# One core, a depthwise convolution and an attention-and-FFN layer: the main stage's order by a place per task, the last product with 128 weight columns, and the first pixels loaded ahead of the build

## The chip, the core and the metric

One core of a Trainium2 chip runs the whole kernel. A core has a tensor engine for matrix products (PE in the profile; its weight loads are listed apart, as PEld), a vector engine (DVE), a scalar engine (ACT), a general engine (POOL) and an engine that only issues transfers (SP). ACT and POOL issue transfers too. Each engine has its own instruction list and works through it in order; the engines meet through semaphores. Sixteen DMA engines move data between DRAM and the on-chip memory (SBUF). The tensor engine writes into eight PSUM banks, which DVE and ACT read.

The metric is device time in microseconds for one execution, the median of three runs.

## What is computed

The input is `x`, 64 images of 55 x 55 pixels with 96 channels. Cut to what matters:

```python
# layer 0: a depthwise 25 x 25 convolution of which 9 x 9 taps less the centre are kept (every third row and column)
lat = conv_general_dilated(x, kernel * mask, strides (1, 1), 'SAME', feature_group_count=96)
x = lat * x + bias + x

# layer 1: tokens t = x as (64, 3025, 96)
n = layernorm(t)
h = relu(bn1(n @ w1.T))                    # 96 -> 192
X = fft(h over the 3025 tokens, ortho)
xr = relu(X.real * rd - X.imag * id + rb)  # rd, id: diagonals, per channel
xi = relu(X.imag * rd + X.real * id + ib)
y = ifft(xr + 1j * xi, ortho).real
t = t + bn2(y @ w2.T)                      # 192 -> 96
# FFN with quantised values: products of fp8 (5, 2), sums rounded to fp16
n = layernorm(t)
h = relu(q16(q16(q8(n) @ q8(W1).T) + q8(b1)))        # 96 -> 384
t = t + q16(q16(q8(h) @ q8(W2).T) + q8(b2))          # 384 -> 96
```

## The kernel before

It has two stages that follow one another.

**The convolution stage** begins with a build. `taps` and a table of selections `sel` are loaded, and 56 groups of small products (L205) make banded weight matrices out of them: one set for the first 48 channels, in `toep` (copied by ACT, L214), one for the other 48, in `later` (copied by DVE, L215). `later` is written to a DRAM scratch `tb` (L217) and comes back into `toep` half-way. Only then, on SP's queue behind the six `tb` transfers, are the first pixels loaded (`load`, L229 to L235, called at L304). Then twelve groups follow, listed at L223 to L225: a half of the channels, a row offset `r` (tiles: 4, 3 and 3) and a half of the images `bh`. Each group goes through its 48 channels in six steps of eight; `compute` multiplies (L253), DVE forms `(lat + 1) * x` (L261), POOL adds the bias (L271). There are six output buffers `buf`. `stores` gives the DMA issues that write a finished buffer to the DRAM scratch `t1`: large ones from ACT's queue (in the last group from SP's too) and small ones from POOL's. Stores are issued a few per step (L326), or at once where the next group needs the buffers (L315).

**The main stage** handles the 64 images one by one as `sequence(b)`, several of them in flight. One sequence is 289 tasks, of which 73 are the tensor engine's:

- load `t` (L549), statistics (L560), layernorm (`layernorm_tasks`), scale (L574), transpose (`pa`, L587, 7 tasks), first product (`ph`, L609, 13 tasks), relu, first transform over 121 tokens (`pf`, L624, 13 tasks), copy, then to DRAM `gd` and back as `gt`;
- the transform's second factor (`dft_r`, `px`, L692, 6 tasks of 32 products with 50 x 64 weights), ACT's three passes (L709), DVE's four (L718) and POOL's two (L725); `project` (`pd`, L767 and L777, 4 tasks of 32 products), `inverse_k1` (`pe`, L797, 4 tasks of 16 products), copies, through DRAM `ed` and back as `e2`;
- the inverse's last factor (`py`, L859, 5 tasks), residual and statistics, layernorm, quantise, transpose in fp8 (`pq`, L913, 7 tasks), up (`pu`, L936, 9 tasks), cast, bias and relu on DVE (L945, L948), quantised to fp8 `hq` by ACT (L960), down (`pw`, L981, 5 tasks of 15 products whose weights are 121 columns of `hq`), cast on ACT (L990), bias on DVE (L995), residual on POOL (L1001) and store.

`px`, `pd` and `pe` are products on a part of the array (64 x 64, or 128 x 64); all others use it whole. An fp32 product is two instruction pairs in the profile, a weight load and a matmul each.

The order of the tasks is set before the program is built. Each `task` has an engine, a cost in us and a place: a formula of the sequence number and of what it is (`at`, `bo`, `co`, `fo`). `ordered` plays the tasks through in time: a task is ready when its predecessors have ended and its buffers are free (`bufs` has their number: 5 of `t`, 4 banks in `psn`, 2 double banks in `psw`), and of the tasks that can start on an engine at nearly the same time the one with the lower place is taken, unless one with a place over `NEAR` higher is ready sooner. For the tensor engine a change of the array's form costs `SWITCH`. What comes out is the order of instructions of each engine, SP included; at run time only the semaphores decide when each one runs.

Of the kernel before, what the change touches and what calls it, by code (L numbers as in the profile page):

```python
# [11 lines left out]
F32 = mybir.dt.float32  # L12
# [9 lines left out]
NTOK = R * R  # L22
# [19 lines left out]
NOB = 6  # L42
SU = 21
# [8 lines left out]

@with_exitstack
def conv_attn_hybrid(ctx, tc, a, out, t1, tb, gds, eds):
# [21 lines left out]
    with ExitStack() as cx:  # L76
# [9 lines left out]
        later = lp.tile([128, CHH, NE * TQ], F32, tag="later", name="later")  # L86
# [47 lines left out]
        for of in (toep, later):  # L134
            nc.gpsimd.memset(of[:, :, : 2 * TQ], 0.0)
            nc.gpsimd.memset(of[:, :, 16 * TQ :], 0.0)
# [61 lines left out]
        for j0 in range(0, TQ, 5):  # L198
            nj = min(5, TQ - j0)
            for e in range(2, 16):  # L200
# [14 lines left out]
                nc.vector.tensor_copy(later[:, :, cols], src[:, CHH:])  # L215
        for c0 in range(0, CHH, CC):
            nc.sync.dma_start(tb[:, c0 : c0 + CC], later[:, c0 : c0 + CC])  # L217
        first.close()

        ob = cx.enter_context(tc.tile_pool(name="c_ob", bufs=NOB))
        groups = [(0, r, bh) for r, bh in ((0, 0), (1, 0), (0, 1), (1, 1), (2, 0), (2, 1))]  # L223
        halfway = groups[-1]
        groups += [(1, r, bh) for bh in range(BH) for r in range(NR)]  # L225
        steps = [(n, c0) for n in range(len(groups)) for c0 in range(0, CHH, CC)]
        xts, bufs_ = {}, {}

        def load(n, c0):  # L229
            half, r, bh = groups[n]  # L230
            c1 = half * CHH + c0
            for m in range(NTS[r]):
                x = xp.tile([128, CC, NBS], F32, tag=f"x{m}", name=f"x{m}_{n}_{c0}")
                nc.sync.dma_start(x, a["xc"][bh, sum(NTS[:r]) + m][:, c1 : c1 + CC, :])
                xts[n, c0, m] = x  # L235
# [39 lines left out]
        def stores(n, m):  # L275

            half, r, bh = groups[n]
            rows_, buf, b0 = TPS[r], bufs_.pop((n, m)), bh * BB
# [3 lines left out]
            for i in range(nr):  # L282
                n0 = (3 * (rows_ * m + i) + r) * R
                large.append((
                    nc.sync if last and i % 2 else nc.scalar,
                    t1[b0 : b0 + BB, half, n0 : n0 + 48, :].rearrange("b (q s) c -> q b (s c)", s=3),
                    buf[at_row(i) : at_row(i) + 16].rearrange("q (b s) c -> q b (s c)", s=3),
                ))


            to = t1[b0 : b0 + BB, half].rearrange("b (y z) c -> y b (z c)", z=R)
# [12 lines left out]
        for step in steps[:2]:  # L304
            load(*step)
        for k, (n, c0) in enumerate(steps):
# [4 lines left out]
            for m in range(nt):  # L311
                compute(n, c0, m)
                if m < early:
                    for queue, to, of in stores(n, m):
                        queue.dma_start(to, of)  # L315
# [4 lines left out]
            if ending:  # L320
                pending = [x for m in range(max(0, early), nt) for x in stores(n, m)]
# [21 lines left out]

    pools = {}
# [15 lines left out]
    tasks, users, edges = [], {}, {}  # L360
    FULL, SWITCH, NEAR, RING = "128x128", 0.09, 0.359, 8
    PLAIN = (FULL, FULL, 0.05, 0.05)

    def task(eng, cost, place, what, after=(), new=(), use=()):
        k = len(tasks)
        tasks.append((eng, cost, place, what, tuple(after), tuple(new), tuple(use) + tuple(h for h, _ in new)))
        for h in tasks[k][6]:
            users.setdefault(h, []).append(k)
        return k

    def ordered(bufs):
# [11 lines left out]
        dma_free, last, landed = 0.0, PLAIN, []  # L383
# [22 lines left out]
        while len(order) < n:  # L406
            best = None
            for eng, q in queue.items():
# [3 lines left out]
                for place, k in q[:60]:  # L412
                    if first is not None and first[0] <= f + 0.2 and place > first[2] + NEAR:
                        break
                    r = max(f, ready_at[k])
                    wanted = [pool for _, pool in tasks[k][5]]
# [33 lines left out]
            else:  # L450
                free[eng] = end[k] = start + cost
            for h, pool in tasks[k][5]:
# [13 lines left out]
        e2=1, xc=2, xq=2, tq=1, hq=1, y16=2, z16=2, o16=2, ot=3, rstda=2, rstdc=2, mean=2, psn=4, psw=2,  # L466
# [4 lines left out]
    def make(h, pool, shape, dt=F32):  # L471
        k = count[pool] = count.get(pool, -1) + 1
        if pool == "tnt":
            live[h] = tnts[k % 2]
        elif pool in ("sm", "sr"):
# [23 lines left out]
    def layernorm_tasks(b, place, what, t, after, mean):  # L499

        st, rstd = (f"st{what}", b), (f"rstd{what}", b)
# [32 lines left out]
        new = [(mean, "mean")] if mean is not None else []  # L534
        k = task("POOL", 1.9 if new else 1.45, place + 0.048, variance, after, new=new, use=[st])
        k = task("ACT", 0.57, place, root, [k])
        k = task("DVE", 0.22, place, inverse, [k], new=[(rstd, f"rstd{what}")])
        return task("POOL", 1.12, place, newton, [k], use=[(rstd)])

    def sequence(b):  # L540
# [4 lines left out]
        def load():  # L545
            tt = make(t, "t", [NJ, 2, NR1, CHH])
            tv = t1[b].rearrange("h (j r) c -> j h r c", r=NR1)
# [3 lines left out]
        loaded = task("SP", (2, 0.41, 4.25), b - 0.85, load, new=[(t, "t")])  # L551
        sta = ("sta", b)
        ks = []
        for q in range(5):
# [9 lines left out]
            ks.append(task("DVE", 0.8, b - 0.6 - 0.214 + 0.06 * q, stats, after, new=new, use=[t] if new else [t, sta]))  # L564
        rstd = layernorm_tasks(b, b - 0.28, "a", t, ks, None)
        g_done = []
        for i in range(7):
            g0, ng = 4 * i, min(4, NR1 - 4 * i)
            at = b + 0.861 * (2 * i - 2.0) / 13
# [24 lines left out]
            k = task("POOL", 0.784 if ng == 4 else 0.31, at - 0.129, scale, [rstd], new=[(xa, "xa")], use=[t, ("rstda", b)])  # L594
            k = task("PE", 0.103 * ng, at, turn, [k], new=[(pt, "psn"), (tnt, "tnt")] + ([(gd, "gd")] if i == 0 else []), use=[xa])
            edges[k] = (FULL, FULL, 0.06, 0.1)
            turned_ = task("ACT", 0.1 + 0.087 * ng, at, turned, [k], use=[pt, tnt])
            ks = []
            for p in range(2 * i, min(2 * i + 2, 13)):
                nq = min(2, NR1 - 2 * p)  # L600
                at = b + 0.861 * p / 13
# [24 lines left out]
                def keep(p=p, nq=nq, pf=pf, g=g):  # L626
# [5 lines left out]
                k = task("PE", 0.326 * nq, at, hidden, [turned_], new=[(ph, "psn"), (h, "h")], use=[tnt])  # L632
                edges[k] = (FULL, FULL, 0.16, 0.16)
                k = task("ACT", 0.107 + 0.137 * nq, at, relu, [k], use=[ph, h])
                first = p % 2 == 0
                k = kj = task("PE", 0.325 * nq, at + 0.074, dft_j, [k] + ([] if first else [kj]), new=[(pf, "psn")] + ([(g, "g")] if first else []), use=[h])
                edges[k] = (FULL, FULL, 0.16, 0.16 * nq)
                ks.append(
                    task("ACT", 0.107 + 0.137 * nq, at + 0.05, keep, [k], use=[pf, g])
                )  # L640

            def put(i=i, g=("g", b, i), g0=g0, ng=ng):
# [7 lines left out]
                task("SP", (2, 0.6, 0.364 * ng), b + (2 * i + 2) / 13, put, ks, use=[("g", b, i), gd])  # L650
# [3 lines left out]
        bo = b + 0.9  # L654
        e_done = []
        gts, fetches = [("gt", b, c) for c in range(4)], []
        for c in range(4):
# [8 lines left out]
            fetches.append(task("SP", (4, 0.33, 2.98), bo - 0.18 + c / 4, fetch, g_done, new=[(gts[c], "gt")], use=[gd]))  # L666

        def spectral(n, kind, c):


            at = bo + 0.876 * n / 6
# [69 lines left out]
            kx = task("PE", 0.94, at, dft_r, after, new=new, use=mine)  # L741
            edges[kx] = ("64x64", "64x64", 0.05, 0.05)
            km = task("ACT", 0.57, at, lambda: affine(m, AF.Abs, 2, 0), [kx], use=[px, m])
            kn = task("ACT", 0.57, at, lambda: affine(nc_, AF.Identity, 4, 5), [kx], use=[px, nc_])
            ka = task("ACT", 0.57, at, lambda: affine(ar, AF.Identity, 2, 0), [kx], use=[px, ar])
            km = task("DVE", 0.57, at, lambda: larger(m, p_(1), m), [km, kn, ka], use=[px, m])
            km = task("DVE", 0.57, at, lambda: larger(m, p_(5), m), [km], use=[px, m])
            kd = task("DVE", 0.57, at, lambda: larger(d1, p_(0), nc_), [kn, ka], use=[px, nc_, d1])
            kn = task("DVE", 0.57, at, lambda: larger(nc_, nrd[:, hh], nc_), [kd], use=[px, nc_])
            kr = task("POOL", 0.99, at - 0.126, real, [km, ka], new=[(s, kind)], use=[ar, m])  # L750
            return s, [kr, task("POOL", 0.99, at - 0.126, imaginary, [kn, kr], use=[d1, nc_, s])]

        def projection(c, at, sm, sr, s_done, e, before):
# [51 lines left out]
            def inverted(pe, k2p):  # L805
# [5 lines left out]
            k = kp = task("PE", 2.2, at, project, s_done, new=[(p, "psn") for p in pds] + [(d, "d") for d in ds_], use=[sm, sr])  # L811
            edges[kp] = ("128x64", "64x64", 0.07, 0.06)
            ks = [
                task("ACT", 0.37, at + 0.02, lambda pd=pd, d=d: projected(pd, d), [k], use=[pd, d])
# [3 lines left out]
            k = task("PE", 0.65, at + 0.07, inverse_k1, ks + before[:1], new=new, use=ds_ + ([e] if x else []))  # L818
            edges[k] = ("64x64", "64x64", 0.05, 0.06)
            return before + [  # L820
                task("ACT", 0.37, at + 0.07, lambda pe=pe, q=q: inverted(pe, q), [k], use=[pe, e])
# [3 lines left out]
        for half in range(2):  # L825
# [3 lines left out]
            for x, (full, f_done) in enumerate(parts):  # L829
                ks = projection(2 * half + x, bo + 0.176 + 0.876 * (3 * half + x + 3) / 6, full, rest, f_done + r_done, e, ks)  # L830
# [11 lines left out]
            e_done.append(task("SP", (4, 0.42, 1.85), bo + (3 * half + 5) / 6, put_e, ks, use=[e, ed]))  # L842


        co = bo + 1.777
# [7 lines left out]
        fetched = task("SP", (1, 1.0, 4.1), co - 0.2, fetch_e, e_done, new=[(e2, "e2")], use=[ed])  # L853
        ks = []
        for q in range(5):
# [22 lines left out]
            at = co + 0.066 * q  # L878
            k = task("PE", 0.81, at, inverse_k2, [fetched], new=[(py, "psn")], use=[e2])
            edges[k] = (FULL, FULL, 0.16, 0.4)  # L880
            k = task("DVE", 0.675, at, residual, [k], use=[py, t])
            new = [(stc, "stc")] if q == 0 else []
            ks.append(task("DVE", 0.8, at + 0.01, stats, [k] + ks[:1], new=new, use=[t] if new else [t, stc]))
        mean = ("mean", b)
        rstd = layernorm_tasks(b, co + 0.25, "c", t, ks, mean)
        fo = co + 0.558
        turned_ = []
        for i in range(7):
            g0, ng = 4 * i, min(4, NR1 - 4 * i)
            xc, xq, pq = ("xc", b, i), ("xq", b, i), ("pq", b, i)  # L890
            at = fo + 0.021 * i
# [253 lines left out]
```

## Time and profile before

| | us |
|---|---|
| median of 3 runs | 4615.11 |
| lowest, highest | 4611.95, 4620.09 |
| the profiled execution | 4654.67 |
| its span, first to last instruction | 4652.9 |
| first product of the convolution (L253) | 85.59 |
| last product of the convolution | 950.2 |
| first product of the main stage (L587) | 1021.70 |

The profiled execution took 39.6 us, 0.9%, more than the median. The profile's own busy time of the tensor engine counts each matmul until its modelled end, so short idle stretches between matmuls are partly covered; idle stretches that remain are put down to what ended them. "issue" is a wait for nothing that the profile shows. The mean granted clock of the tensor engine over the span was 0.965; it stands at 1.0 or 0.5 at any moment, and the mean of a stretch says how much of it was spent at 0.5.

### The profile page before, as it was taken

What the parts mean: (1) busy time and instruction counts of PE and PEld (TensorE: products, weight loads), DVE (VectorE), ACT (ScalarE), POOL (GpSimd) and SP (SyncE); (2) the same over time, 40 slices, a digit from 0 to 9 for tenths busy, and PEclk for the clock granted to TensorE, in tenths of its full rate; (3) what the DMA queues carried; (4) which work ended last, traced back from release to release, by engine and by line L of the source; (5) the groups of instructions that cost most, each with busy time, mean ns of one, the idle gap of its engine ahead of it and who ended that gap; (6) DMA issues with size and microseconds to landing.
All of it is one profiled execution on the core that took longest, in us unless ns stands there. A gap on an engine that the chain in (4) does not pass through costs nothing.

```text
span 4652.9 us, 194788 instructions
## 1 busy us (share of the span) xinstructions
PE 4284.9 (92%) x83314; PEld 3569.2 (77%) x83314; DVE 3280.7 (71%) x7232; ACT 2963.2 (64%) x5947; POOL 3087.5 (66%) x4209
## 2 busy tenths in 40 slices
PE   7998798939999999999999999999999999999987
PEld 6998798937777777777777777777777777777775
DVE  4544354424888877877887788788787878788776
ACT  2000000017888888887887888888887888788875
POOL 1766576745666767766776666677766666677655
PEclk8999899969999999999999999999999999999996
DMA  4678888786666666766676666676666666667662
GB/s 162 166 193 204 245 197 207 190 185 165 165 171 178 179 177 178 181 177 169 180 183 169 169 174 179 172 185 180 176 183 169 177 174 176 171 179 183 177 162 71
DMA packets 572798, 823.14 MB, mean 177 GB/s; under 512 B 62127, under 2 KB 470276, under 8 KB 570268
## 3 DMA queue, kind: packets, MB, share of 16 engines
q1 hardware_dynamic: 442704, 736.10, 58.7%
q10 hardware_dynamic: 113036, 64.71, 7.1%
q0 software_dynamic: 16192, 9.86, 1.1%
q8 instruction: 655, 10.73, 1.0%
q14 instruction: 211, 1.73, 0.1%
HBM read 419.45 MB, written 390.64 MB: 174 GB/s over the span
## 4 chain that ended last, share of the span: by engine, by line
PE 71%; DVE 7%; DMA 7%; ACT 6%; issue 5%; POOL 2%; ACTq 2%; SPq 0%; POOLq 0%; DVEq 0%
PE pl L253 13%; PE pf L624 9%; PE ph L609 9%; PE pd L767 7%; PE px L692 7%; PE pw L981 5%; PE py L859 4%; PE pd L777 4%; PE pu L936 4%; PE pe L797 3%; PE pa L587 3%; DMA x<-in_xc_dram 2%; DMA t<-buf 2%; DVE y L945 2%; PE pq L913 2%
## 5 line engine op out<-in xcount | busy, mean ns | idle before, releaser
L253 PE MATMUL pl<-x,toep 128*64 128x96 f32 (+1 forms) x18432 | 790.1, 250 | 99.0 <-DVE buf L261 41.2
L253 PEld LDWEIGHTS pl<-x,toep 128*64 128x64 f32 (+1 forms) x18432 | 783.4, 137 | 105.7 <-issue 55.7
L945 DVE CAST y<-pu 128x1008 f16<-128x1008 f32 (+1 forms) x576 | 689.2, 1202 | 224.6 <-PE pu L936 220.5
L261 DVE SCALAR_TENSOR_TENSOR buf<-pl,x 121x384 f32<-121x384 f32 (+1 forms) x480 | 390.1, 842 | 499.0 <-PE pl L253 314.3
L609 PEld LDWEIGHTS ph<-w1e,tnt 97*121 97x121 f32 x3200 | 543.3, 185 | 210.9 <-issue 64.4
L960 ACT ACTIVATE hq<-z 128x1008 fp8e5<-128x1008 f16 (+1 forms) x576 | 601.2, 1050 | 156.7 <-DVE z L948 156.3
L718 DVE SCALAR_TENSOR_TENSOR m<-px,par,m 128x400 f32<-128x400 f32 x768 | 480.8, 626 | 286.3 <-ACT ar L709 201.6
L609 PE MATMUL ph<-w1e,tnt 97*121 97x192 f32 x3200 | 665.1, 330 | 12.9 <-ACT e L806 11.4
L271 POOL TENSOR_TENSOR buf<-buf,cbias 121x768 f32<-121x768 f32 (+1 forms) x240 | 434.1, 1821 | 363.9 <-DVE buf L261 252.1
L624 PE MATMUL pf<-h,f 121*128 121x384 f32 (+1 forms) x1664 | 664.8, 484 | 4.9 <-ACT h L618 2.6
L521 ACT ACTIVATE sm_s_a<-sm_v_a,eps 121x25 f32<-121x25 f32 x64 | 20.3, 318 | 959.0 <-POOL sm_v_a L512 956.6
L574 POOL TENSOR_TENSOR xa<-t,rstda 121x384 f32<-121x384 f32 (+1 forms) x448 | 348.2, 780 | 419.7 <-PE pa L587 411.7
L692 PE MATMUL px<-m,gt 50*64 50x50 f32 x24576 | 456.4, 220 | 63.1 <-issue 59.8
L692 PEld LDWEIGHTS px<-m,gt 50*64 50x64 f32 x24576 | 416.0, 136 | 122.0 <-issue 105.2
L725 POOL TENSOR_TENSOR sm<-ar,m 128x400 f32<-128x400 f32 x256 | 270.9, 1058 | 353.6 <-DVE m L718 296.4
L767 PE MATMUL pd<-w2e,sm 128*64 128x96 f32 x8192 | 415.7, 254 | 30.9 <-ACT g L628 18.0
L628 ACT COPY g<-pf 128x384 f32<-128x384 f32 (+1 forms) x832 | 385.6, 467 | 85.5 <-PE pf L624 70.6
L1001 POOL TENSOR_TENSOR ot<-t,o 121x480 f32<-121x480 f32 x320 | 374.3, 1177 | 91.2 <-DVE o L995 91.2
L618 ACT ACTIVATE h<-ph 121x384 f32<-121x384 f32 (+1 forms) x832 | 389.8, 488 | 68.3 <-PE ph L609 61.6
L948 DVE TENSOR_SCALAR z<-y,b1q 128x1008 f16<-128x1008 f16 (+1 forms) x576 | 418.9, 732 | 11.4
L767 PEld LDWEIGHTS pd<-w2e,sm 128*64 128x64 f32 x8192 | 358.6, 139 | 76.0 <-ACT g L628 22.5
L981 PEld LDWEIGHTS <-hq 128*121 128x121 fp8e5 x4800 | 315.9, 142 | 77.1 <-issue 37.6
(115 smaller groups left out, 8367.2 us busy)
## 6 DMA issues: line engine op xcount, KB each, us to landing
gd<-g SPq DMA_DIRECT2D x768, 192.0 KB
gt<-gd SPq DMA_DIRECT2D x512, 288.0 KB
x<-in_xc_dram SPq DMA_DIRECT2D x240, 384.0 KB
t<-t SPq DMA_DIRECT2D x64, 1050.0 KB
out_dram<-ot SPq DMA_DIRECT2D x320, 210.0 KB
t<-buf ACTq DMA_DIRECT2D x211, 288.0 KB
ed<-e SPq DMA_DIRECT2D x384, 150.0 KB
ed<-e SPq DMA_DIRECT2D x128, 131.2 KB
```

The costliest lines, as they stand in the source:

```text
L253: nc.tensor.matmul(pl[p : p + width, cc * NBS : (cc + 1) * NBS], toep[:, c0 + g + cc, o : o + width], xts[n, c0, m + d][:, g + cc, :], sta ...
L261: nc.vector.scalar_tensor_tensor(buf[:px, :, c0 + g : c0 + g + CG].rearrange("p n c -> p c n"), pl[:px, : CG * NBS].rearrange("p (c n) -> ...
L271: nc.gpsimd.tensor_tensor(part, part, cbias[:px, c1 : c1 + CC].unsqueeze(1).to_broadcast([px, NBS, CC]), ALU.add)
L609: nc.tensor.matmul(x[:NJ, q * H : (q + 1) * H], live[tnt][:, g * NJ : (g + 1) * NJ], w1e, start=True, stop=True,)
L624: nc.tensor.matmul(x[:, : nq * H], f1, live[h][:, : nq * H], start=True, stop=True)
L692: nc.tensor.matmul(x[to : to + 64].rearrange("p (q r n) -> p q r n", q=2, r=2)[:, k2p, :, o : o + NR1], y[rows, k % KC, c0 : c0 + 64], m1[ ...
L718: nc.vector.scalar_tensor_tensor(live[out_], view(px)[:, :, 256 : 256 + KC * NR1], scale, live[than], ALU.mult, ALU.max)
L767: nc.tensor.matmul(y[k % 2][64 * k2p : 64 * k2p + 64, k // 2 * CH : (k // 2 + 1) * CH], full[:, k, 64 * k2p : 64 * k2p + 64], w2e[:, 0, :] ...
L945: nc.vector.tensor_copy(live[y16][:, :n], live[pu][:, :n])
L948: nc.vector.tensor_scalar(make(z16, "z16", [128, 1024], F16)[:, :n], live[y16][:, :n], b1q[:, k : k + 1], 0.0, ALU.add, ALU.max,)
L960: nc.scalar.activation(live[hq][:, k, n0 : n0 + n], live[z16][:, :n], AF.Copy, saturate=False)
L981: nc.tensor.matmul(p[:NJ, g * CH : (g + 1) * CH], live[hq][:, k, n0 : n0 + NJ], w2q[:, k, :], start=(k == 0), stop=(k == 2),)
```

## The change

It has four parts, and none of them changes the arithmetic.

**The order.** The place formulas go. A table `PLACES` has one number for each of a sequence's 289 tasks, and the place is the sequence number plus it. `NEAR` goes from 0.359 to 0.5. `ordered` learns one more thing: the two `bias` tasks of DVE (`alone`) and all tasks of POOL exclude one another in time. Costs in two places are others: `down` 0.66 instead of 0.84, the second `bias` 0.33 instead of 0.6. The small layernorm tiles are listed among the buffers (`small=2`).

```diff
-    FULL, SWITCH, NEAR, RING = "128x128", 0.09, 0.359, 8
+    FULL, SWITCH, NEAR, RING = "128x128", 0.09, 0.5, 8
-    def task(eng, cost, place, what, after=(), new=(), use=()):
+    def task(eng, cost, what, after=(), new=(), use=()):
         k = len(tasks)
+        place = k // len(PLACES) + PLACES[k % len(PLACES)]
...
                     r = max(f, ready_at[k])
+                    if eng == "POOL":
+                        r = max(r, shared)
+                    elif k in alone:
+                        r = max(r, free["POOL"])
...
-            x = task("DVE", 0.4, at, bias, [x], new=[(z16, "z16")], use=[y16])
+            x = task("DVE", 0.4, bias, [x], new=[(z16, "z16")], use=[y16])
+            alone.add(x)
```

**Down with 128 weight columns.** `hq` is no longer a buffer of 3025 columns out of a pool but one fixed tile `hidden8` with seven columns more, which POOL clears once. Each product of `down` loads 128 columns instead of 121; the seven extra rows of its result are not read.

```diff
+    hidden8 = late.tile([128, 3, NJ * NR1 + 7], F8, tag="hidden8", name="hidden8")
+    nc.gpsimd.memset(hidden8[:, :, NJ * NR1 :], 0.0)
...
-                            p[:NJ, g * CH : (g + 1) * CH],
-                            live[hq][:, k, n0 : n0 + NJ],
+                            p[:, g * CH : (g + 1) * CH],
+                            live[hq][:, k, n0 : n0 + 128],
                             w2q[:, k, :],
```

**Pixels ahead of the build.** The loads of the first two steps are SP's first issues, ahead of `taps` and `sel`. The first groups change places: `r = 1` (three tiles) before `r = 0` (four). `later` is three tiles of 16 channels, so DVE copies each group of the build in three pieces, 168 copies instead of 56.

```diff
-        later = lp.tile([128, CHH, NE * TQ], F32, tag="later", name="later")
+        later = [lp.tile([128, CPL, NE * TQ], F32, tag=f"later{k}", name=f"later{k}") for k in range(CHH // CPL)]
+        groups = [(0, r, bh) for r, bh in ((1, 0), (0, 0), (1, 1), (0, 1), (2, 0), (2, 1))]
...
+        for step in steps[:2]:
+            load(*step)
         kt = selp.tile([128, CH], F32, tag="kt", name="kt")
         nc.sync.dma_start(kt, a["taps"])
...
-                nc.vector.tensor_copy(later[:, :, cols], src[:, CHH:])
+                for k, of in enumerate(later):
+                    c1 = CHH + CPL * k
+                    nc.vector.tensor_copy(of[:, :, cols], src[:, c1 : c1 + CPL])
```

**The step from one stage to the other.** `t1` is two tensors, one for each half of the images. In the last group no store is issued inside the loop; all follow its last product. The loads of sequences 0 and 1 are issued from POOL's queue, in one piece each, and no longer from SP's.

```diff
-                if m < early:
+                if m < early and n + 1 < len(groups):
...
+            if b < 2:
+                nc.gpsimd.dma_start(tt, tv)
+                return
             for p0, p1 in split(NJ):
                 nc.sync.dma_start(tt[p0:p1], tv[p0:p1])
```

## The prediction

> **What bounds the kernel now.** I read the page's first part, then stretches of 100 us (the convolution is tensor-bound but for its ends, the main stage steady from 1200 to 4500 us), then that stage alone: its busy times and what the tensor engine waited for.
>
> ```profile
> span 4652.9 us, 194788 instructions
> PE 4284.9 (92%) x83314; PEld 3569.2 (77%) x83314; DVE 3280.7 (71%) x7232; ACT 2963.2 (64%) x5947; POOL 3087.5 (66%) x4209
> ...
> q8 instruction: 655, 10.73, 1.0%
> ```
>
> ```profile
> 1200.00:4500.00 3300.00, 3157.88 (x59362) 2518.97 (x59358) 2650.75 (x6153) 2722.13 (x5462) 2309.53 (x3437) 0.99 0.68 176
> ```
>
> The columns are length, busy PE, PEld, DVE, ACT and POOL, clock, DMA share, GB/s. PE is busy 95.7% of the stage; ACT, next, 82.5%. PE bounds it. The 4425 `pw` matmuls of this stretch, 75 a sequence, make 59 sequences: 55.9 us each. Idle: 142.1 us, 2.4 a sequence. Its largest releasers:
>
> ```profile
> PE px L692 <- issue: 53.8, 58, 2.3
> PE pd L767 <- ACT g L628: 18.0, 30, 0.8
> PE pd L777 <- issue: 16.5, 14, 2.9
> ...
> PE pd L767 <- issue: 10.4, 11, 2.5
> PE pe L797 <- issue: 8.6, 10, 1.6
> PE pw L981 <- issue: 5.5, 6, 1.4
> ```
>
> With 2.0 of `pq`, 96.8 us are "issue": no operand was missing. The queue named instruction explains it: 10.73 MB over 83314 weight loads and as many matmuls is 64 bytes each, a packet is 16.4 KB, so PE's own list arrives in pieces of 256. The waits sit in `px`, `pd` and `pe`, where instructions are densest (128 in the 1.0 us of a `px` task, against 4 in the 0.65 us of a `pf`).
>
> The weight loads, and the matmul of the build:
>
> ```profile
> L981 PEld LDWEIGHTS <-hq 128*121 128x121 fp8e5 x4800 | 315.9, 142 | 77.1 <-issue 37.6 <-ACT hq L960 15.2 <-ACT d L786 1.2
> L913 PEld LDWEIGHTS <-xq 121*96 121x96 fp8e5 x1600 | 124.1, 127 | 78.2 <-POOL xq L904 31.8 <-issue 16.9 <-POOL sr L725 0.5
> L936 PEld LDWEIGHTS <-w1q 96*128 96x128 fp8e5 x1152 | 102.5, 101 | 47.3 <-issue 20.3 <-DVE nc L718 2.7
> L205 PE MATMUL pt<-kt,sel 128*64 128x96 f32 x1064 | 45.4, 250 | 0.0
> ```
>
> The 128-column fp8 load takes 101 ns, less than the 96-column one. Three stretches of the timeline (start, length, what):
>
> ```profile
> 2522.19 0.81 PE L609 MATMUL ph<-w1e,tnt 97*121 97x192 f32 x4
> 2522.85 0.81 PE L624 MATMUL pf<-h,f 121*128 121x384 f32 x2
> ...
> 2523.92 0.81 PE L609 MATMUL ph<-w1e,tnt 97*121 97x192 f32 x4
> 2524.67 1.15 PE L692 MATMUL px<-m,gt 50*64 50x50 f32 x64
> ```
>
> ```profile
> 62.18 5.66 SPq L217 DMA_DIRECT2D tb<-later  x6
> 67.88 70.90 SPq L234 DMA_DIRECT2D x<-in_xc_dram  x22
> ...
> 85.59 0.58 PE L253 MATMUL pl<-x,toep 128*64 128x96 f32 x4 [24.24 <-DMA x<-in_xc_dram]
> ```
>
> ```profile
> 989.96 26.40 SPq L549 DMA_DIRECT2D t<-t  x10
> ...
> 1003.90 4.09 DVE L560 BATCH_NORM_STATS2 sta<-t 121x6 f32<-121x96 f32 x25 [52.65 <-DMA t<-t]
> ...
> 1021.70 1.85 PE L587 MATMUL pa<-ident,xa 121*96 121x121 f32 x8 [71.28 <-POOL xa L574]
> ```
>
> First: the same `ph` task is followed after 0.66 us by a task on the whole array, after 0.75 by one on a part: 0.1 us for a change of form. Second: the first pixels, issued behind `tb`, cost PE 24.2 us. Third: 71.3 us between the stages.
>
> **The change, part by part.** Gains negative, for 64 sequences.
>
> *Down.* Fifteen `pw` matmuls follow one another at 56 ns (on the timeline two tasks of 15 take 1.68 us): with 96 moving columns and 121 weight columns the weights set the pace. If their load stops doing so, the moving columns do: 45.4/1064 = 43 ns in L205, also 96 columns. 15 x 13 ns = 0.2 us a task, 320 tasks: -64. Bounds 0 and -64. The `w1q` row is the nearest, so nearly all: -58, the rest lost where PE waits anyway. Seven more rows of result cost nothing: columns set the pace.
>
> The Trainium skill ("TensorE: Matmul & The Clock Gate", Weight-path perf modes) has a fast weight load that needs 128 weights and a dtype that is not FP32, as here; by it the full -64. The same page (Back-to-back issue gap) speaks against: pairs of load and matmul are said to sustain some 81 ns at 128 columns, so nothing would be gained. The 56 ns of this trace are already below that.
>
> *Instruction pieces.* I laid PE's tasks of both programs out in their final order, gave each its start-to-start time from the timeline (`px` 0.97, `pd` 2.18, `pe` 0.71, `ph` and `pf` 0.65, `py` 0.81, `pu` 0.43, `pa` 0.10 and `pq` 0.054 a product) and cut the list every 256 instructions. A piece that holds less work than a fetch needs leaves PE waiting. With a fetch of 3.9 us the shortfalls of before's order make 1.65 us a sequence, as measured (96.8/59 = 1.64). In the new order they are 0.34: the longest run of part-array tasks falls from 640 instructions to 448, and 10% of pieces hold under 3.9 us instead of 30%. 1.31 x 64: -84. At 3.5 us it is 0.87 against 0.09 (-50); all that was measured gone would be -105.
>
> *Changes of form.* Shorter runs are more runs: 16 changes a sequence instead of 11. 5 x 0.1 x 64: +32. Bounds 0 (hidden under waits) and +40.
>
> *Waits for other engines.* Now 45.3 us of the stage, 0.77 a sequence, from a fixed order on each engine. Bounds: all gone, -49; or one more of the kind of the `pd` wait (18.0/30 = 0.6) a sequence, +38. I take +19, since `pd` tasks now come in pairs more often (1.0 a sequence, was 0.5) and PE's faster work leaves ACT less slack. The exclusion of DVE's biases and POOL is only the planner's; L948's 732 ns may fall, off PE's path.
>
> *Clock.* 0.99 over 3300 us is 33 us lost. If it follows the idle time, which the terms above halve, -15. Bounds 0, -33.
>
> *Start.* SP issues six pixel loads (384 KB each) ahead of `sel`: 2.4 MB at the 291 to 376 GB/s of the first transfers is 6 to 8 us. But PE began the build at 15.95, held by the parameters' chain, so I take 1 us. DVE's pieces (80 columns; a 96-column copy, L147, takes 256 ns, three 0.77) stay under PE's 0.82 a group; if that cover goes, tenths of a us on 56 groups. PE then starts at once, not 24.2 later. Two steps of three tiles last 19 us, to about 82; step three's pixels lie behind `tb` as the first did (85.5), so 5 back. And a four-tile group now follows a three-tile one once more: such a group took 88.7 us where the first group, as large, took 81.9; 4 of these 7. -24 + 1 + 5 + 4 = -14; bounds -24 and +5.
>
> *Between the stages.* No gain. On POOL's queue the first two loads stand behind 18 small stores and six clearings, and in the changed program's list of waits they wait for all 16 store semaphores, to the last group's last store; so do SP's next loads. `hidden8` moves the `t` tiles up into the memory of the output buffers. Before, the first load went out at 989.96, ahead of the last stores' landing. It will go some 5 to 10 us later, but with fewer stores beside it and two queues; POOL's biases are no longer held between stores. DVE still takes 15 statistics of sequence 1 ahead of sequence 0's reciprocal. 0, bounds -15 and +15.
>
> Sum: -58 - 84 + 32 + 19 - 15 - 14 + 0 = -120. Profiled 4654.7 would be 4535; the median stands 39.6 lower, 4615 - 120 = 4495.
>
> **Rivals.**
> - *The gain moves into other waits.* Fetch and clock gains (99) come back as waits for ACT, at 82.5% already: -58 + 32 - 14 = -40, 4575. For it: every in-order engine follows the same fixed order. Against: 17.5% slack. 0.20.
> - *The wide load isn't faster* (unaligned columns, 121 apart): -62, 4553. Against: the `w1q` row. 0.12.
> - *Slower: PSUM banks.* Two `pd` tasks in a row hold all four banks of `psn`, and the `pe` behind them needs two; ACT frees two with copies of 0.49 each, queued behind a 1.05 us `hq` pass. 2.0 us, one to two times a sequence; at 3 us it is +192 - 120 = +72, 4687. It decides from 1.9 us a sequence on. For it: pairs double. Against: the copies are due while the second `pd` (2.2 us) runs. 0.10.
>
> **Numbers.** The forecast, 4405 to 4545, has 0.55; no change 0.03 (within 0.2%, 9 us, about what a measurement here can tell from none). Faster 0.55 + 0.20 + 0.12 = 0.87, slower 0.10. The range takes in the two milder rivals: 4405 (all fetch waits, most of the others and the clock gained) to 4585.
>
> **What would show it.** Right: `pw` loads near 100 ns and 15 matmuls in 0.65 us; "issue" in the stage under 35 us; a sequence at 54 us; L253 beginning near 63; 66 to 78 us between the stages. Wrong: `pw` still at 56 ns; `pd` or `pe` waiting for ACT by over 100 us; ACT over 90% with PE under 95%.

## The result: 1.5% slower, and the profile after

The changed kernel takes 4690.18 us (median of 4 runs, 4670.88 to 4704.34) against 4617.6 us for the kernel before (4 runs, 4611.95 to 4626.22): ratio 1.0153, 95% interval 1.011 to 1.0196. The forecast was 4495, the range 4405 to 4585. The profiled execution took 4670.88 us. Its page begins:

```profile
span 4669.1 us, 195011 instructions
## 1 busy us (share of the span) xinstructions
PE 4267.8 (91%) x83314; PEld 3481.7 (75%) x83314; DVE 3194.6 (68%) x7344; ACT 2948.6 (63%) x5947; POOL 3082.9 (66%) x4216
```

PE is busy 17 us less than before and the span is 16 us longer: the products did get cheaper, and PE stood still for longer. The two profiles understate the loss: the kernel before was profiled in an execution 37 us above its median, the changed kernel in its fastest, 19 us below its median, so the spans differ by 16 us where the medians differ by 73. The stretch 1200 to 4500 us, with the same columns as before:

```profile
1200.00:4500.00 3300.00, 3117.09 (x58606) 2420.95 (x58601) 2534.08 (x6117) 2673.52 (x5401) 2279.79 (x3408) 0.98 0.66 174
```

PE went from 95.7% to 94.5% of the stage, and every other engine fell too. No other engine became the bound; something holds all of them. The list of PE's waits in that stretch names it (us in total, times, longest):

```profile
PE py L906 <- DMA e<-ed: 110.4, 54, 3.6
PE px L740 <- issue: 27.7, 29, 2.1
PE px L740 <- DMA gt<-gd: 16.7, 33, 1.1
PE py L906 <- ACT hidden L1004: 10.9, 5, 2.2
PE pe L845 <- issue: 8.6, 7, 2.3
```

"Issue" fell from 96.8 to 41.6 us over all its rows, as the order was meant to make it. The first row is new: `py`, the inverse's last factor, waits 2.0 us in nearly every sequence (54 of 59) for `e2`, the spectrum that comes back from DRAM. Before, no row named `py`. The place of it, first on PE, then on SP's queue (start, length, what):

```profile
2539.23 0.60 PE L980 MATMUL pu<-tq,w1q 96*128 96x512 fp8e5 x2
2539.66 0.81 PE L659 MATMUL ph<-w1e,tnt 97*121 97x192 f32 x4
2542.52 1.84 PE L906 MATMUL py<-e,i 128*121 128x480 f32 x4 [2.04 <-DMA e<-ed]
```

```profile
2527.46 1.27 SPq L694 DMA_DIRECT2D gd<-g  x2
2528.77 2.67 SPq L885 DMA_DIRECT2D ed<-e  x4
2532.90 1.24 SPq L694 DMA_DIRECT2D gd<-g  x2
2535.49 0.71 SPq L896 DMA_DIRECT2D e<-ed  x1
```

Read them together. `put_e` (L885, the task that writes `e` to `ed`) begins the moment the put of `gd` (L694) ahead of it has been issued, and the fetch (L896, which brings `ed` back as `e2`) comes behind another such put. It went out at 2535.49, and `py` started at 2542.52, 7.0 us later. Both puts of `gd` stand so in all of 45 sequences looked at. In the kernel before they do in 23 of 45, and in the others no put of `gd` stands in these places. One of the 23, and the `py` that belongs to it:

```profile
2542.64 1.24 SPq L644 DMA_DIRECT2D gd<-g  x2
2543.98 2.48 SPq L837 DMA_DIRECT2D ed<-e  x4
2548.39 1.24 SPq L644 DMA_DIRECT2D gd<-g  x2
2550.08 0.70 SPq L849 DMA_DIRECT2D e<-ed  x1
```

```profile
2561.07 0.97 PE L859 MATMUL py<-e,i 128*121 128x480 f32 x2
```

Here PE comes to `py` 11.0 us after the fetch, and no wait is marked. The weight loads of the down matmuls (`pw`):

```profile
L1025 PEld LDWEIGHTS <-hidden 128*128 128x128 fp8e5 x4800 | 231.5, 99 | 57.9 <-ACT hidden L1004 13.7 <-issue 1.8 <-ACT tq L962 0.3
```

99 ns, was 142; fifteen `pw` in a row take 0.638 us from the first start to the next task's, were 0.844. The start and the gap between the stages, on PE:

```profile
63.46 11.40 PE L288 MATMUL pl<-x,toep 128*64 128x96 f32 x272
75.67 0.88 PE L288 MATMUL pl<-x,toep 128*64 128x96 f32 x16 [0.80 <-issue]
88.83 6.36 PE L288 MATMUL pl<-x,toep 128*64 128x96 f32 x92 [12.29 <-DVE buf L296]
...
997.46 1.85 PE L638 MATMUL pa<-ident,xa 121*96 121x121 f32 x8 [83.26 <-POOL xa L625]
```

The convolution starts at 63.5 as forecast, then stands 12.3 us, since DVE's first write to an output buffer waits until 87.98 for the store of `later` to `tb`: the buffer takes the memory of `later`. Between the stages 83.3 us pass, were 71.3.

For what follows I use a steadier measure than a cut in time: the mean time from the first `py` of the sixth sequence to that of the 59th, with the time in that stretch for which the trace shows PE's granted clock at 0.5 (there is no other value below 1).

| kernel | ratio to before (95%) | us a sequence | us at half clock |
|---|---|---|---|
| before | 1 | 55.61 | 71.7 |
| after | 1.0153 (1.011 to 1.0196) | 56.14 | 119.5 |
| e1 down alone | 0.9991 (0.997 to 1.0013) | 55.42 | 71.7 |
| e2 old order in the changed kernel | 0.995 (0.993 to 0.997) | 55.14 | 47.8 |
| e3 e's transfers first | 0.9818 (0.9794 to 0.9843) | 53.53 | 37.5 |
| e4 py later | 0.9957 (0.9933 to 0.998) | 54.86 | 64.9 |
| e5 as e3, 121 columns | 0.9901 (0.9863 to 0.9939) | 54.09 | 37.5 |
| e6 after, 121 columns | 1.0141 (1.0105 to 1.0176) | 56.22 | 88.6 |
| e7 wait filled | 1.0053 (1.0032 to 1.0074) | 55.48 | 47.8 |
| e8 as e3, first loads on SP | 0.9799 (0.9757 to 0.9842) | 53.62 | 41.0 |
| e9 new start alone | 1.0006 (0.999 to 1.0022) | 55.56 | 51.2 |
| e10 only put_e first | 1.0091 (1.0071 to 1.011) | 55.71 | 102.4 |
| e11 only the fetch first | 1.0049 (1.0027 to 1.0072) | 55.82 | 122.9 |

The ratios are medians over several runs; the two right columns are one profiled execution each. The chips differ a little (the kernel before took 4618 to 4640 us on them), so kernels are compared by ratio.

### The profile page after: what moved, and what is told of

Same layout as the page of the kernel before. It is cut to its first block, busy times and chain, and to the rows that moved or that the text cites. A ratio compares the mean times of both kernels' runs of the same rounds, so it can differ in the third digit from the quotient of the medians.

```text
span 4669.1 us, 195011 instructions
## 1 busy us (share of the span) xinstructions
PE 4267.8 (91%) x83314; PEld 3481.7 (75%) x83314; DVE 3194.6 (68%) x7344; ACT 2948.6 (63%) x5947; POOL 3082.9 (66%) x4216
## 4 chain that ended last, share of the span: by engine, by line
PE 71%; DMA 20%; issue 3%; ACT 2%; ACTq 2%; SPq 1%; DVE 1%; POOL 1%; POOLq 0%; DVEq 0%
PE pl L288 13%; PE ph L659 9%; PE pf L674 9%; DMA e<-ed 9%; PE px L740 7%; PE pd L815 7%; PE py L906 6%; DMA gt<-gd 4%; PE pd L825 4%; PE pa L638 4%; PE pe L845 3%; PE pu L980 3%; DMA x<-in_xc_dram 2%; DMA ed<-e 2%; PE pw L1025 2%
## 5 line engine op out<-in xcount | busy, mean ns | idle before, releaser
L288 PE MATMUL pl<-x,toep 128*64 128x96 f32 (+1 forms) x18432 | 784.7, 249 | 66.0 <-DVE buf L296 47.8
L659 PE MATMUL ph<-w1e,tnt 97*121 97x192 f32 x3200 | 634.5, 332 | 6.1 <-issue 2.7
L1004 ACT ACTIVATE hidden<-z 128x1008 fp8e5<-128x1008 f16 (+1 forms) x576 | 593.1, 1052 | 60.2 <-DVE z L992 59.8
L740 PE MATMUL px<-m,gt 50*64 50x50 f32 x24576 | 472.4, 222 | 50.5 <-issue 30.7
L766 DVE SCALAR_TENSOR_TENSOR d<-px,par,nc 128x400 f32<-128x400 f32 x384 | 241.1, 628 | 367.6 <-ACT ar L757 290.9
L906 PE MATMUL py<-e,i 128*121 128x480 f32 x640 | 334.2, 624 | 127.0 <-DMA e<-ed 116.0
L674 PEld LDWEIGHTS pf<-h,f 121*128 121x128 f32 x1664 | 291.9, 195 | 171.2 <-issue 50.9
L556 POOL TENSOR_TENSOR sm_d_a<-sta 121x25 f32<-121x25 f32 x64 | 45.2, 706 | 540.1 <-DVE sta L612 540.1
L815 PE MATMUL pd<-w2e,sm 128*64 128x96 f32 x8192 | 398.2, 250 | 1.6 <-issue 0.8
```

The lines of the kernel that those rows point to most:

```text
L288: nc.tensor.matmul(pl[p : p + width, cc * NBS : (cc + 1) * NBS], toep[:, c0 + g + cc, o : o + width], xts[n, c0, m + d][:, g + cc, :], sta ...
L659: nc.tensor.matmul(x[:NJ, q * H : (q + 1) * H], live[tnt][:, g * NJ : (g + 1) * NJ], w1e, start=True, stop=True,)
L674: nc.tensor.matmul(x[:, : nq * H], f1, live[h][:, : nq * H], start=True, stop=True)
L740: nc.tensor.matmul(x[to : to + 64].rearrange("p (q r n) -> p q r n", q=2, r=2)[:, k2p, :, o : o + NR1], y[rows, k % KC, c0 : c0 + 64], m1[ ...
L766: nc.vector.scalar_tensor_tensor(live[out_], view(px)[:, :, 256 : 256 + KC * NR1], scale, live[than], ALU.mult, ALU.max)
L815: nc.tensor.matmul(y[k % 2][64 * k2p : 64 * k2p + 64, k // 2 * CH : (k // 2 + 1) * CH], full[:, k, 64 * k2p : 64 * k2p + 64], w2e[:, 0, :] ...
```

## The experiments

Theory 1: the new order puts `py` ahead of the landing of `e2`; the wait, and the half clock that follows it, make the whole loss. Theory 2: the new order costs through its changes of form and its waits elsewhere. Theory 3: the new start and what it moved costs.

**e1, down alone**: the kernel before, with the padded tile and 128 columns.

```diff
-                            p[:NJ, g * CH : (g + 1) * CH],
-                            live[hq][:, k, n0 : n0 + NJ],
+                            p[:, g * CH : (g + 1) * CH],
+                            live[hq][:, k, n0 : n0 + 128],
```

> The kernel before, with the down matmuls alone changed to 128 weight columns (padded hidden8 tile); order and start are those of before. Both theories agree here, it prices the part: down took 0.844 us per 15 matmuls before and 0.638 us in the changed kernel, 5 groups x 64 sequences, so -66 us if PE sets the stage: 4545 to 4560 against 4617.6, ratio 0.985 to 0.988. If the wide load's gain were swallowed by other waits (rival: ACT becomes the bound) the time would stay above 4600, ratio over 0.996.

4623.4 us against 4621.0: nothing, where 4545 to 4560 was expected. The time lies where the rival put it, over 4600, but ACT did not become the bound: it is busy 82.6% of the stage, was 82.5%. The 15 matmuls did fall to 0.638 us. PE's waits from 1200 to 4500 us rose from 138.4 to 167.3 us, "issue" among them from 96.8 to 113.5, waits for ACT, POOL and the rest from 41.6 to 53.8. The first rows, and two that were not there before:

```profile
PE px L697 <- issue: 52.4, 57, 2.5
PE pd L782 <- issue: 24.6, 12, 3.4
...
PE pa L592 <- ACT o L995: 6.3, 13, 0.7
...
PE pf L629 <- ACT o L995: 3.0, 8, 0.8
```

The forecast's rival "the gain moves into other waits" is what happens to part of this gain in the old order: the waits rose by 28.9 us, where 59 sequences of five such tasks, each 0.206 us shorter, should save 61. My reading is that faster matmuls use up the instruction pieces sooner and that the tasks behind them reach ACT's work too early; no run tests it, and where the rest of the gain went stays open.

**e2, the old order in the changed kernel**: places, costs and planner of before; new start, new order of groups and 128 columns stay.

```diff
-        place = k // len(PLACES) + PLACES[k % len(PLACES)]
+    def task(eng, cost, place, what, after=(), new=(), use=()):
...
-            k = task("PE", 0.81, inverse_k2, [fetched], new=[(py, "psn")], use=[e2])
+            k = task("PE", 0.81, at, inverse_k2, [fetched], new=[(py, "psn")], use=[e2])
```

> The changed kernel with the main stage's order made by the places, costs and planner of before: keeps the new start, the new convolution order and the 128 columns. Theory 1 (the new order puts the first py of a sequence ahead of the landing of its e2, 2.2 us of wait a sequence and the clock's loss behind it): without that order the main stage falls to that of e1, and the start's 24 us are kept: 4520 to 4540, ratio 0.979 to 0.983, no wait of py for DMA. Rival (the loss comes with the new start, the loads of the first two sequences on POOL's queue or the moved memory, and its clock): still above 4617, ratio over 1.

4601 us, ratio 0.995. It missed the expected 4520 to 4540, because down is worth nothing there (e1), but it clears the start of the loss: theory 3 wanted more than 4617. The new order as a whole, with its wait, costs 1.0153 - 0.995 = 2.0% of 4617, 94 us.

**e3, e's transfers first**: on SP's queue alone the second `put_e` and the fetch are each issued ahead of the put of `gd` that stood before them.

```diff
+    plan = ordered(bufs)
+    for k in [k for k in plan if tasks[k][3].__name__ in ("put_e", "fetch_e") and k % len(PLACES) != 136]:
+        at = plan.index(k)
+        j = max(i for i in range(at) if tasks[plan[i]][0] == "SP")
+        if tasks[plan[j]][3].__name__ == "put":
+            plan.insert(at, plan.pop(j))
     with tc.manual_schedule():
-        for k in ordered(bufs):
+        for k in plan:
```

> The changed kernel; on SP's queue alone the second put of e and the fetch of e are each issued ahead of the one gd put that stands before them. No other engine's order is touched. Theory 1: the gd put holds put_e back by 1.0 us and the fetch by 1.2 us, so e2 lands about 2 us earlier, py's waits for DMA in 1200 to 4500 us fall from 110 us to under 30 us and the time by 100 to 140 us, with the clock at 0.99: 4550 to 4590 us, ratio 0.985 to 0.994. Rival 2 (the new order costs through its 16 changes of form a sequence and its waits elsewhere, the py wait is only where PE's slack shows): the wait moves to another line, 4650 us or more, ratio over 1.007.

4541.8 us, ratio 0.9818: 0.0335 below the changed kernel's ratio, 155 us of 4617, faster than the kernel before and faster than the 4550 to 4590 expected. No product and no other engine's order was touched. SP's queue on the timeline, and the row of waits that was 110.4:

```profile
2528.85 1.66 SPq L885 DMA_DIRECT2D ed<-e  x4
2530.55 1.42 SPq L694 DMA_DIRECT2D gd<-g  x2
2533.75 0.71 SPq L896 DMA_DIRECT2D e<-ed  x1
```

```profile
PE py L906 <- DMA e<-ed: 8.6, 7, 5.0
```

Two puts of `gd` out of the way, and `py` no longer waits. Theory 2 falls: the new order's forms and its other waits are all still in e3.

**e4, py later**: the first two `py` of a sequence and their residuals go behind the `pf`, `pa` and `px` that follow them.

```diff
+    plan, per = ordered(bufs), len(PLACES)
+    for b in range(B - 1):
+        at = plan.index((b + 1) * per + 137)
+        moved = [k for k in plan[:at] if k in (b * per + 184, b * per + 181)]
+        stay = [k for k in plan[: at + 1] if k not in moved and k != b * per + 182 and k != b * per + 185]
+        back = [k for k in plan[: at + 1] if k in (b * per + 182, b * per + 185)]
+        plan = stay + moved + back + plan[at + 1 :]
```

> The changed kernel; in each sequence the first two py (and their residuals) are put behind the dft_j, the turn and the px that follow them, 2.0 us of PE work by the planner's costs. SP's order is untouched. Theory 1: the 2 us of work cover the transfer, py's DMA wait falls from 110 us in the stage to under 30, 4550 to 4590 us, ratio 0.985 to 0.994. Rival 2 (order costs elsewhere): 4650 or more, ratio over 1.007.

4602.7 us, ratio 0.9957: 0.02 below the changed kernel's, yet short of what was expected. The wait for `e2` left the list, and its first row became

```profile
PE pf L674 <- ACT h L668: 70.8, 58, 1.5
```

The `pf` that now runs first needs a relu that ACT ends 1.2 us too late for it (70.8/58). The wait for the transfer is gone, and a shorter one, for ACT, stands in its place.

**e10 and e11, one lock at a time**: e3's edit for `put_e` alone, then for the fetch alone.

```diff
-    for k in [k for k in plan if tasks[k][3].__name__ in ("put_e", "fetch_e") and k % len(PLACES) != 136]:
+    for k in [k for k in plan if tasks[k][3].__name__ == "put_e" and k % len(PLACES) != 136]:
```

> e3 with only the second put of e moved ahead of its gd put; the fetch of e stays behind the next one. By the trace of the changed kernel the gd put ahead of put_e costs 1.0 us, and the one ahead of the fetch issues 1.24 us but part of that lies inside the 3.4 us in which the fetch waits for put_e's landing anyway (3.37 us from put_e's last issue to the fetch before, 3.67 after). Theory (the block at put_e is what counts): about 0.3 us of 2.3 is lost again, 4545 to 4575, ratio 0.984 to 0.990. Rival (both blocks count alike): half of e3's gain, 4600 to 4630, ratio 0.996 to 1.002.

4672.3 us, ratio 1.0091: both expectations missed, since little was gained. SP's queue shows why, and PE's row what came of it:

```profile
2533.97 1.81 SPq L885 DMA_DIRECT2D ed<-e  x4
2536.12 5.08 SPq L694 DMA_DIRECT2D gd<-g  x4
2541.65 0.71 SPq L896 DMA_DIRECT2D e<-ed  x1
```

```profile
2549.08 1.84 PE L906 MATMUL py<-e,i 128*121 128x480 f32 x4 [1.55 <-DMA e<-ed]
```

Now two puts of `gd` stand between `put_e` and the fetch, 5.08 us from the first issue to the last: the second of them waits for ACT's copy of the next `g`. Medians over 45 sequences, in us:

| from, to | before | after | e10 | e11 | e3 |
|---|---|---|---|---|---|
| last `pe`, to the end of ACT's last copy of `e` | 0.89 | 2.35 | 2.36 | 2.36 | 2.36 |
| that, to the first issue of `put_e` | -0.35 | 0.97 | -0.73 | 0.97 | -0.74 |
| issuing `put_e` | 2.20 | 2.50 | 1.72 | 2.49 | 1.69 |
| its last issue, to the fetch | 3.37 | 3.67 | 6.02 | 3.30 | 3.37 |
| the fetch, to the first `py` | 11.38 | 7.46 | 7.60 | 7.49 | 8.35 |

The second to fifth rows sum to 14.6 in the changed kernel and to 14.6 in e10: what `put_e` gains, the fetch loses behind the put.

> The counterpart of e10: only the fetch of e is moved ahead of its gd put, put_e stays behind its own. In e10 the fetch, with two gd puts ahead of it of which the second waits for ACT's copy of g, went out 6.02 us after put_e's last issue, and the whole way from e's last copy to py was the same 14.6 us as in the changed kernel. Theory (two locks in a row: put_e's issue and the gd put ahead of the fetch open at about the same time, so either alone frees nothing): the fetch waits for put_e's landing, 3.4 us after its last issue instead of 3.67, 0.3 us a sequence = 20 us with the clock's share, 4655 to 4690, ratio 1.006 to 1.014. Rival (the fetch's place alone is the lock): most of e3's gain, 4550 to 4600, ratio under 0.996.

4661.6 us, ratio 1.0049: just under the theory's 1.006, its interval reaching over it; the rival is out. Of ratio e10 gains 0.006 on the changed kernel, e11 0.010, both edits together 0.0335. Two locks in a row: the fetch waits for the landing of `put_e`, and for the put of `gd` ahead of it, and these open at about the same time (without the put ahead of it the fetch goes out 3.30 us after the last issue of `put_e`, with it 3.67).

**e7, the wait filled**: 1.7 us of useless products on constants ahead of the first `py`, in its PSUM tile, which `py` then overwrites.

```diff
+                y = make(py, "psn", None)
+                if q == 1:
+                    for _ in range(2):
+                        nc.tensor.matmul(
+                            y[:NJ, :512],
+                            i2,
+                            m2[:, :8, :].rearrange("p k n -> p (k n)"),
+                            start=True,
+                            stop=True,
+                        )
```

> The changed kernel with two matmuls of 512 columns on constants put ahead of the sequence's first py, into the same PSUM tile, which py then overwrites: 1.7 us of useless PE work where PE waits 2.0 us for e2. Theory 1 with the clock: between the sixth and the 59th sequence the half-clock time was 119.5 us in the changed kernel against 37.5 in e3, which is 41 us of work lost in 53 sequences; with PE kept busy in the wait it comes back to 40 to 60 us and the time falls by 30 to 50 us, 4640 to 4660, ratio 1.004 to 1.010. Rival (the half clock has nothing to do with the wait, or costs nothing): no change or slower, 4690 to 4710, ratio 1.015 or more.

4643.6 us, ratio 1.0053, as expected: 1.0% faster than the changed kernel with more work on PE. The row of waits fell to

```profile
PE py L916 <- DMA e<-ed: 29.6, 37, 2.3
```

and the half-clock time from 119.5 to 47.8 us. At half clock half of the time is lost: 71.7/2 = 35.9 us over 53 sequences, 0.68 each; measured 56.14 - 55.48 = 0.66. So the clock is a cost of its own behind the wait. What `py` alone paid is in the busy time of its line from 1200 to 4500 us (columns: length, PE, PEld, clock, DMA share, GB/s), first the changed kernel, then e7:

```profile
1200.00:4500.00 3300.00, 307.44 (x590) 106.02 (x590) 0.98 0.66 174
```

```profile
1200.00:4500.00 3300.00, 285.66 (x600) 102.01 (x600) 0.99 0.67 176
```

521 ns a record against 476, with ten records a sequence 0.45 us of the 0.66: `py`, which runs first after the wait, takes much of it.

**e5 and e6, 121 columns again**: e3 and the changed kernel with e1's edit undone.

> e3 (changed kernel, e's transfers ahead of the gd puts) with the down matmuls back at 121 weight columns. Asks what the 128 columns are worth once the new order has no wait for e2: alone, in the old order, they were worth 0 (ratio 0.997 to 1.0013). Theory A (the old order gave it back in instruction transfers and ACT waits, of which the new order has half: issue 44 us against 114): 5 x 0.2 us x 64 = 66 us lost, 4595 to 4615, ratio 0.994 to 0.999. Theory B (the wide load is worth nothing in the span in any order): 4542 within 10, ratio 0.980 to 0.985.

> The changed kernel with 121 weight columns, and its wait for e2 left in. Two of the five down groups of a sequence lie between the last pe and the first py, where PE waits for e2: there slower downs only shorten the wait. Theory A: 3 x 0.2 us x 64 = 40 us slower than the changed kernel's 4690, so 4720 to 4750, ratio 1.021 to 1.029. Theory B: 4690 within 15, ratio 1.012 to 1.018.

e5 4579.6 us, ratio 0.9901; e6 4688.1 us, ratio 1.0141. With the wait in place the 128 columns are worth nothing (1.0141 against 1.0153), with the wait gone 0.8%, 38 us. In e6 the wait of `py` for `e2` is 83.3 us instead of 110.4 and the half-clock time 88.6 instead of 119.5: slower down matmuls only shorten the wait. I had expected 40 us for e6 and 66 for e5's loss. e6 fell to theory B (within 15 us of the changed kernel); e5 lies between the two theories, with A right in its sign and B wrong. In e3 the waits that are not "issue" are 60.4 us, in e5 40.5: part of the gain goes into these.

**e8 and e9, the start and the gap between the stages**: e3 with the first two loads on SP's queue, and the changed kernel with the old order and 121 columns.

```diff
-            if b < 2:
-
-                nc.gpsimd.dma_start(tt, tv)
-                return
```

> e3 with the loads of the first two sequences back on SP's queue in two pieces each. Between the stages 85 us passed in e3 against 71 in the kernel before. If the move of these loads to POOL's queue makes that difference: 70 to 75 us between the stages and 4525 to 4535, ratio 0.978 to 0.981. Rival (the memory of t, which hidden8 moved into the store buffers' place, makes it): 85 us stays, 4542 within 10.

> The changed kernel with the old order and 121 weight columns: what is left is the new start, the convolution's new order of groups, the split t1 and the first two loads on POOL's queue. e2 against e1 puts that part at 4601 - 4623 = -22 us: 4595 to 4605, ratio 0.993 to 0.997. If the wide load does count beside the new start (rival: e1's nothing was an accident of its run), e9 would be 15 us or more slower than e2's 4601: 4616 or more, ratio 0.998 or more.

In e8 69.0 us passed between the stages instead of 85.2, so the loads' queue, not the memory, made the difference: in the ten traces with these loads on POOL's queue the gap is 80.3 to 88.6 us. In the time it doesn't show: 4535.7 us, ratio 0.9799 (0.9757 to 0.9842), against e3's 0.9818. In the profiled execution of e8 the convolution ended later, at 932 us (920 in e3). Its trace shows 75.1 us of that stage at half clock against 58.0 in e3, which makes 8.6 of the 12 us; why the clock fell there is open. e9 gives 4631.0 us against 4632.1: the new start alone is worth nothing that can be told, although its first product is 22 us earlier: 12.3 of these go into the wait for `buf`, and 9.0 into the gap between the stages (80.3 us, was 71.3). e2 is 0.4% below e1 and 0.56% below e9, so start and down together give more than the two alone. That stays open: e9 ran on another chip than e1 and e2.

## Why the prediction was wrong

The step that failed is "Waits for other engines": 45.3 us of the stage, bounded at +38 by "one more of the kind of the `pd` wait", taken at +19. The waits that are not "issue" went from 41.6 to 140.0 us in the stage, 1.67 us a sequence or 107 for 64, and the one that came, 110.4 us, is not for an engine but for a transfer. I had laid PE's tasks out in the new order and asked of it only how dense the instructions are and how often the form changes. I had not set the same list against the transfers. In the kernel before, `py` came 11.38 us after the fetch, with nearly 4 us to spare over the 7.5 that the changed kernel shows, where `py` stands waiting. The new order spent this on both sides. The transfer comes later: ACT's copies of `e` end 1.5 us later, `put_e` starts 1.3 us later behind a put of `gd`, and its issue and the fetch take 0.6 longer. And PE comes to `py` sooner: from the last `pe` to the first `py` it took 17.6 us (median of 45 sequences), and now 17.2, of which 1.9 is waiting, so 2.3 us less lie between. 3.4 later and 2.3 sooner, less the 3.9 to spare, leave 1.8 us, about the wait that came.

The second step that failed is "Clock", -15, "if it follows the idle time". It did follow the idle time, and that rose: half-clock time 71.7 to 119.5 us in 53 sequences, (119.5 - 71.7)/2/53 = 0.45 us a sequence, +29 for 64. That may well be low: the four executions of the changed kernel, from the fastest to the slowest, show mean clocks of 0.964, 0.960, 0.957 and 0.955, and the profiled one is the first.

The others, against what the runs showed:

- *Down*, -58: the matmul's price was right (0.844 to 0.638 us), its worth in the span was not. It depends on what waits behind: 0 in the old order (e1) and beside the wait (e6), 38 us once the wait is gone (e5 against e3).
- *Instruction pieces*, -84: "issue" from 96.8 to 41.6 us in the stage, 0.94 us a sequence, -60. The mechanism holds, and the traces show it more plainly than the forecast did: number PE's weight loads, matmuls and sequencer instructions in order of time and divide by 256, and each "issue" wait of the stage, 103 before and 43 after, leaves the remainder 193 or 194. So they all stand at one place of a piece of 256. The size lies within the bounds, and "under 35" was missed.
- *Changes of form*, +32: the traces have 10.9 changes a sequence between tasks on a part of the array and tasks on the whole of it before, and 15.7 after (1200 to 4300 us). The price holds: from its start to the next task's, a `py` takes 0.81 us ahead of a task on the whole array and 0.90 ahead of a `px` or `pe`. 4.8 x 0.1 x 64 is +31, an estimate; no run has the changes alone.
- *Start*, -14, and *Between the stages*, 0: the first product came as forecast. The sum left out the wait for `buf`, 12.3 us, and between the stages 83.3 us came instead of 66 to 78, from the loads' place on POOL's queue (e8). Both parts together measured 0 in e9, and some -19 beside the 128 columns (e2 against e1).

By the right price for the wait the sum closes, in us a sequence of the profiled executions. From the kernel before to the changed one: down -1.03 (5 x 0.206), "issue" -0.94, changes of form +0.5, other waits +1.67, clock +0.45, together +0.65; measured 56.14 - 55.61 = +0.53. (The terms lean on one another: in e6, without the -1.03, the wait is shorter.) From the changed kernel to e3 the sequence falls by 2.61 us: (110.4 - 8.6)/59 = 1.73 of wait and (119.5 - 37.5)/2/53 = 0.77 of clock. And e3's 53.53 us a sequence is near the 54 that the forecast expected of the order; its 4541.8 us lie in the forecast's range.

Of the rivals, the PSUM banks gave nearly the measured time (4687), and were not the cause: `pe` waits for ACT in no row of the changed kernel's stage, and the `pd` wait for ACT's `g`, 18.0 us before, is gone. That the number fits is luck. "The gain moves into other waits" is right for down alone. What the forecast named as a sign of being wrong (`pd` or `pe` waiting for ACT, ACT over 90%) did not come; it didn't name a transfer.

On the 128 columns, the rule of the Trainium skill ("TensorE: Matmul & The Clock Gate", Weight-path perf modes) holds here: 0.638 us for 15 is 43 ns each, with starts 121 columns apart. The 81 ns of its section Back-to-back issue gap, given for 128 moving columns, are shown by no row: the nearest is `pq` with 121 moving columns, at 54 ns a product.

## What to carry to other kernels

When an order is planned for the bounding engine, follow each round trip through DRAM in it: from the last product to the copy, the issue, its place in the queue, the landing and the first use, each with its measured time, and compare with the work left in between. A queue that issues in order makes a transfer wait for whatever the one ahead of it waits for, and moving one of two such blocks gains little while the other stands (here 0.6 and 1.0%, both together 3.35%). A cheaper instruction is worth what the next wait leaves of it: here 0 or 38 us for the same edit.

## What the runs showed of the hardware

A wait of 2 us on PE can cost more than 2 us. In the changed kernel, from 1200 to 4300 us, 54 gaps between PE's matmuls were over 1.5 us, and within 7 us of the beginning of 24 of them a stretch at clock 0.5 began. The trace has 31 such stretches there. They last 3.41 us, or twice that.

The Trainium skill ("TensorE: Matmul & The Clock Gate", HAM oscillation) gives idle gaps of over about 3.4 us as what throttles the clock; here gaps of 1.5 to 2.5 us were followed by it in 17 of 43 cases. The half of the throttled time that the page takes as the penalty agrees with e7: 0.68 us worked out, 0.66 measured.
